# Order of first loads, of routing and scatter, router by quarters and a shared expert in 11 parts, in a two-layer kernel on one Trainium2 core

## The chip, the core and the metric

The kernel runs on one core of one Trainium2 chip. The metric is device time in microseconds (us) of one execution. The engines are TensorE (PE in the profile; PEld is its loading of weights), VectorE (DVE), ScalarE (ACT), GpSimd (POOL) and SyncE (SP), which only issues DMAs here. ScalarE and GpSimd issue DMAs too. Each engine takes its instructions strictly in order.

## The reference, cut to what matters

Two layers over 4 sequences of 512 tokens with 512 channels, all in float32. Each of the four blocks gets the normalised input, and its normalised output is added to the residual x.

```python
# layer 0, attention: a state space model of 1024 channels
conv = silu(causal_depthwise_conv4(x @ in_proj.T))
dt = softplus(einsum(conv, dt_w) + dt_b); s = scan(exp(dt*A), dt*B*conv)
x0 = ((C*s + D*conv) * sigmoid(x @ gate_proj.T)) @ out_proj.T
# layer 0, feed forward: 8 experts, 2 per token, and a shared expert of 704 columns
logits = x @ gate_weight.T; top 2 of softmax(logits)
y = sum over the 2: w * (silu(x @ gate_e) * (x @ up_e)) @ down_e      # 352 columns each
y = y + (silu(x @ sg) * (x @ su)) @ shared_down                        # 704 columns
# layer 1, attention: gated delta rule, 16 heads of 128, alpha and beta = sigmoid(x @ Wa + ba), sigmoid(x @ Wb + bb)
# layer 1, feed forward: a switch over 8 experts of width 32 per sequence
```

## The kernel before

The program has three stages, one after the other on each engine: `state_space` (L366), `experts` (L766) and `upper_layer` (L1023). A tile is 128 tokens by 512 channels (16 tiles, `x[0]` to `x[15]`); a sequence has four.

`state_space` and `upper_layer` write their work as operations with an engine, an assumed cost and a due time; `Plan.sequence` (L153) simulates the engines with these costs and fixes one order for each engine, also for SP's DMAs. `experts` is written in program order; the framework under it places each engine's instructions in an order of its own, and waits are by semaphores.

**First loads.** SP loads `x[0]` to `x[3]` (L250). ScalarE issues the constants (L252), the parameters `prm` (L369), `w_in`, `w_gate` and `w_out` (L376, L379), 14 DMAs in all. The planner then has SP load `x[4]` and on (L548) and write zeros to the buffer `xg` of routed rows in 13 DMAs (`clear`, L448), with due times only. At most 8 loads of the two queues are in flight: each later one waits for the landing of an earlier one. A sequence begins with statistics (L415), normalising (L431), transposes (L559) and copies of these by ScalarE (L569); then come the projections `w_in` and `w_gate` (L443), the convolution (L606, L617), steps through a small DRAM round trip (L481 to L530, L662), the scan and the output projection.

**Experts.** `route(b)` (L828) normalises and transposes the four tiles of sequence b and makes the router's logits with 16 matmuls of 8 columns (L836). `shared(b)` (L799) is the shared expert for one sequence: the 704 columns lie as two halves of 352 with chunks of 128, 128 and 96 (`FCH`), so 6 chunks, each with a gate and an up product of 4 matmuls (L312, 512 tokens wide), Silu on ScalarE (L808) and a multiply on VectorE (L809); then for each of the four tiles 6 matmuls down (L814), a copy (L822) and a store. The up products use 4 banks of PSUM (`mm`), the down products 2 (`tr`). Sequences 0 and 1 go route, shared, route, shared (L853); then routes 2 and 3, the top 2 and the places of all rows (L856 to L936), the scatter of 16 tiles (L939: VectorE normalises a tile into one of two buffers, GpSimd sends it to its two places by indirect DMAs, L944), and shared expert 2 (L1002). After that come 39 tiles of routed rows (`raised`, `lowered`, L954 and L980), whose expert's number is read on SP (L956) before its weights are fetched. The memory pools of this stage wait for the whole pool before them.

**Upper layer.** `shared_last` (L1139) is the shared expert of sequence 3 as planned operations; `begin(b)` (L1226) gathers the routed rows, adds, normalises and transposes, and makes alpha and beta with 16 matmuls of 32 columns and 4 for the biases (`both`, L1288). Then 8 pairs of heads for each sequence, the switch and its experts.

Of the kernel before, what the change touches and what calls it, by code (L numbers as in the profile page):

```python
# [18 lines left out]
P = 128  # L19
# [10 lines left out]
E, F, NX = 8, 352, 10  # L30
# [15 lines left out]
def _constants():  # L46
# [12 lines left out]
    parts["ones"] = np.ones((P, P))  # L59
    parts["key"] = np.broadcast_to(E - np.arange(E), (P, E))  # L60
# [174 lines left out]
def network(ctx: ExitStack, tc: tile.TileContext, a: dict, out: bass.AP):  # L235
# [16 lines left out]
    nc.scalar.dma_start(const, a["const"])  # L252
# [50 lines left out]
    def residual(pool, i, y):  # L303

        mv, rs = stats([y], EPS, "r")
        yn = pool.tile([P, D], F32, tag="xn", name="yn", bufs=2)
        normalise(yn, y, mv, rs, 0)
        nc.gpsimd.tensor_tensor(x[i], x[i], yn, ALU.add)

# [3 lines left out]

    def conv_silu(pool, dst, p, w, bias):

        cv = pool.tile([P, S], F32, tag="cv", name="cv", bufs=2)
        nc.scalar.activation(cv, p, AF.Identity, bias=bias, scale=w[:, 3:4])
        for j in range(1, 4):
            nc.vector.scalar_tensor_tensor(
                cv[:, j:], p[:, : S - j], w[:, 3 - j : 4 - j], cv[:, j:], ALU.mult, ALU.add  # L320
            )
        sg = pool.tile([P, S], F32, tag="sg", name="sg", bufs=2)
        nc.scalar.activation(sg, cv, AF.Sigmoid)
        nc.gpsimd.tensor_tensor(dst, cv, sg, ALU.mult)
# [41 lines left out]
    def state_space():  # L366
        with tc.tile_pool(name="w1", bufs=1) as wp, tc.tile_pool(name="s1", bufs=1) as sp:
            prm = wp.tile([P, a["p1"].shape[1]], F32, tag="prm", name="prm")
            nc.scalar.dma_start(prm, a["p1"])  # L369
# [3 lines left out]
            for w, name in ((w_in, "w_in"), (w_gate, "w_gate")):  # L373
                src = a[name].rearrange("(k p) c -> p k c", p=P)
                for k in range(KD):
                    nc.scalar.dma_start(w[:, k, :], src[:, k, :])  # L376
            src = a["w_out"].rearrange("(k p) d -> p k d", p=P)
            for k in range(0, NCT, 2):
                nc.scalar.dma_start(w_out[:, k : k + 2, :], src[:, k : k + 2, :])  # L379
# [26 lines left out]
            in_there = op("LD", 9.0, -9.0, lambda: None, [there])  # L406
            gate_there = op("LD", 9.0, -9.0, lambda: None, [in_there])
            out_there = op("LD", 9.0, -9.0, lambda: None, [gate_there])
# [39 lines left out]
            def clear(j, due):  # L448

                tiles = xg.rearrange("(j p) d -> p j d", p=P)  # L450
                op(
                    "SP",
                    0.42,
                    due,
                    lambda: nc.sync.dma_start(
                        tiles[:, j : j + 3, :], zero.unsqueeze(1).to_broadcast([P, 3, D])
                    ),
                )
# [78 lines left out]
            def sequence(b, due):  # L537
                xT = slot("xT", [P, KD, S], 2)
                turned = []
                for i in range(TPB):  # L540
                    xi = x[b * TPB + i]
                    ld = there
                    if b:
                        ld = op(
                            "SP",
                            0.42,
                            due - 0.8,
                            lambda xi=xi, i=i: nc.sync.dma_start(xi, x_in[b * TPB + i]),  # L548
                            landing=3.5,
                        )  # L550
# [43 lines left out]
                for half in range(2):  # L594
# [3 lines left out]
                    for ct in cts:  # L598
# [38 lines left out]
                        )  # L637
                    kept, dd = decay_steps(half, X, made, at + 0.15)
# [118 lines left out]
            for j in range(NG // 3):  # L757
                clear(3 * j, 0.8 + 0.2 * j)
# [7 lines left out]
    def experts():  # L766
        later = ctx.enter_context(ExitStack())
        lp = later.enter_context(tc.tile_pool(name="t2", bufs=1, side="right"))
        with (
            tc.tile_pool(name="w2", bufs=2) as wp,  # L770
            tc.tile_pool(name="s2", bufs=1) as sp,
            tc.tile_pool(name="e2", bufs=2) as ep,
        ):
            wr = sp.tile([P, KD, E], F32, tag="wr", name="wr")
# [24 lines left out]
            def shared(b, xT):  # L799
                acts = []  # L800
                for gu, _ in halves:
                    for lo, n in FCH:
                        act = lp.tile([P, S], F32, tag="act", name="act", bufs=2 * len(FCH))
                        pg, pu = ps("mm"), ps("mm")
                        project(pg[:n], lambda k: gu[:, k, lo : lo + n], xT)
                        project(pu[:n], lambda k: gu[:, k, F + lo : F + lo + n], xT)
                        sl = lp.tile([P, S], F32, tag="sl", name="sl", bufs=1)
                        nc.scalar.activation(sl[:n], pg[:n], AF.Silu)  # L808
                        nc.vector.tensor_tensor(act[:n], sl[:n], pu[:n], ALU.mult)  # L809
                        acts.append((act, n))  # L810
                for r in range(TPB):
                    pd = ps("tr")
                    for f, (act, n) in enumerate(acts):
                        nc.tensor.matmul(  # L814
                            pd,
                            lhsT=act[:n, r * P : (r + 1) * P],
                            rhs=halves[f // len(FCH)][1][:n, f % len(FCH), :],
                            start=f == 0,
                            stop=f == len(acts) - 1,
                        )  # L820
                    y = ep.tile([P, D], F32, tag="y", name="y")
                    nc.scalar.copy(y, pd)  # L822
                    nc.sync.dma_start(ys[b * TPB + r], y)
# [4 lines left out]
            def route(b):  # L828

                home = sp if b < B - 1 else lp  # L830
                xT = home.tile([P, KD, S], F32, tag="xT", name="xT")
                norms.append(norm_transposed(sp, xT, b))
                lg = ps("sq")[:, : TPB * E]
                for i in range(TPB):
                    for k in range(KD):
                        nc.tensor.matmul(  # L836
                            lg[:, i * E : (i + 1) * E],
                            lhsT=xT[:, k, i * P : (i + 1) * P],
                            rhs=wr[:, k, :],
                            start=k == 0,  # L840
                            stop=k == KD - 1,
                        )
# [5 lines left out]
            halves = []  # L848
            for j in range(2):
                gu = lp.tile([P, KD, 2 * F], F32, tag=f"gu{j}", name="gu")  # L850
                dn = lp.tile([P, len(FCH), D], F32, tag=f"dn{j}", name="dn")
                halves.append(fetch(gu, dn, a["gu"][j], a["dn"][j]))
            for b in range(B - 2):  # L853
                shared(b, route(b))
            xT = [route(b) for b in range(B - 2, B)]
# [83 lines left out]
            for i in range(NT):  # L939
                xn = sp.tile([P, D], F32, tag="xn", name="row", bufs=2)  # L940
                mv, rs = norms[i // TPB]
                normalise(xn, x[i], mv, rs, i % TPB)
                for k in range(2):
                    put = nc.gpsimd.indirect_dma_start(  # L944
                        out=xg,
                        out_offset=bass.IndirectOffsetOnAxis(ap=places[k][:, i : i + 1], axis=0),
                        in_=xn,
                        in_offset=None,
                        bounds_check=NG * P - 1,
                    )  # L950
                    tc.declare_no_dep(put.ins, group="put", reason="places are distinct")
                    tc.add_to_no_dep_group("put", put.ins)

            def raised(j):  # L954
# [3 lines left out]
                    a["gu"][bass.DynSlice(v + 2, 1)].rearrange("o d f -> (o d) f"),  # L958
                    a["dn"][bass.DynSlice(v + 2, 1)].rearrange("o f d -> (o f) d"),
# [42 lines left out]
            shared(B - 2, xT[0])  # L1002
# [6 lines left out]
            pool=lp, close=later.close, xT=xT[1], halves=halves, places=places, gates=gates  # L1009
# [13 lines left out]
    def upper_layer(first):  # L1023
        with (
# [56 lines left out]
            def one(v, cc):  # L1081
                return v[:, cc * P : (cc + 1) * P]
# [56 lines left out]
            def shared_last(due):  # L1139

                acts, ops = [], []
                xT, halves = first["xT"], first["halves"]
# [4 lines left out]
                def product(p, w, k, rhs, due, after, slots, stop):  # L1147
                    return op("PE", 0.88, due, lambda: mm(p(), w(), rhs(), k == 0, stop), after, slots)

                for n in range(2 * len(FCH)):  # L1150
                    gu = halves[n // len(FCH)][0]
                    at, width = FCH[n % len(FCH)]
                    act, sl = held("act", 2 * len(FCH)), held("sl", 1)
                    d, done, banks = due + 0.65 * n, [], []
                    for lo in (at, F + at):
                        p, last = bank("mm"), None
                        for k in range(KD):
# [4 lines left out]
                                lambda p=p, gu=gu, k=k, lo=lo, w=width: mm(  # L1162
                                    p()[:w], gu[:, k, lo : lo + w], xT[:, k, :], k == 0, k == KD - 1
# [6 lines left out]
                    last = op(  # L1170
                        "ACT",
                        0.63,
                        d,
# [1272 lines left out]
```

## Time and profile before

| what | us |
|---|---|
| median of 3 runs (lowest to highest) | 3107.18 (3105.93 to 3120.01) |
| the profiled execution, its time | 3114.02 |
| its span, first to last instruction | 3112.3 |
| state space, until the last output projection | 0 to 400.9 |
| experts until the first routed tile | 409.0 to 654.7 |
| routed tiles | 654.7 to 984.4 |
| upper layer | 984.4 to 3112.3 |

The granted TensorE clock was 0.958 of full speed on average, in the records either 1.0 or 0.5. In the page, "x13191" is a number of instructions; a float32 matmul makes two records. Section 2 cuts the span into 40 slices of 77.8 us, one digit each, with 9 for 90% or more. A line of a group has the line of the code, the engine, the operation, what is written from what, the shapes, the count, the total busy us, the mean ns of one, and the idle time of the engine before it with what ended that. Matmuls overlap, so the mean ns of one is longer than its share of the time. A line of waits has who waited for whom, the total us, the times and the longest. A line of a timeline has the start in us, how long it took, the engine, the line of the code and the operation, and in brackets the idle time before it and its releaser; "ACTq" is ScalarE issuing DMAs. A line of windows has the stretch, its length, for each engine the busy us and the count, then the granted clock, the DMA engines' busy share and GB/s.

### The profile page before, as it was taken

How to read it: one execution, taken by the hardware profiler on the slowest of the kernel's cores; microseconds unless marked ns; L12 is line 12 of the kernel's file. 1: busy time of each engine (PE TensorE's matmuls, PEld its weight loads, DVE VectorE, ACT ScalarE, POOL GpSimd, SP SyncE). 2: the span in 40 equal slices, each digit the busy share in tenths (PEclk: the TensorE clock that was granted, in tenths of full speed). 3: DMA queues.
4: the chain of work that ended last, by engine and by line, in shares of the span. 5: the costliest groups of instructions: out<-in, count | busy, mean ns of one | idle time of the engine just before them, and what ended most of it. 6: DMA issues, size and time to landing. Idle time of an engine off the chain costs nothing. (4 is left out here: it accounts for less than half of the span.)

```text
span 3112.3 us, 38963 instructions
## 1 busy us (share of the span) xinstructions
PE 2897.8 (93%) x13191; PEld 1623.0 (52%) x13191; DVE 1873.7 (60%) x4648; ACT 1149.7 (37%) x2398; POOL 678.7 (22%) x853
## 2 busy tenths in 40 slices
PE   6899989989999999999998989999989999999976
PEld 2344444445554455655554546555656564656532
DVE  3676730211112466777768785678877678867556
ACT  3454301111111234444444434445544544544530
POOL 0222310210001212332132232122232222221133
PEclk9899989899999999999999999899999999999998
DMA  6111120469996343443345442335443345433333
GB/s 259 56 36 42 42 72 17 153 233 321 319 316 211 88 104 93 118 102 95 77 123 161 110 114 62 80 103 166 115 130 92 90 106 139 122 75 79 84 115 115
DMA packets 288970, 383.81 MB, mean 123 GB/s; under 512 B 127586, under 2 KB 127970, under 8 KB 288514
## 3 DMA queue, kind: packets, MB, share of 16 engines
q1 hardware_dynamic: 274640, 346.07, 38.3%
q0 software_dynamic: 5120, 16.78, 1.6%
q10 hardware_dynamic: 9010, 18.46, 1.6%
q8 instruction: 105, 1.72, 0.2%
q14 instruction: 95, 0.78, 0.1%
HBM read 320.38 MB, written 60.82 MB: 122 GB/s over the span
## 5 line engine op out<-in xcount | busy, mean ns | idle before, releaser
L1085 PE MATMUL mm<-xT,wh 128*128 128x512 f32 x1536 | 775.1, 605 | 3.7 <-issue 3.0
L1448 DVE SCALAR_TENSOR_TENSOR cv<-mm,prm,cv 128x511 f32<-128x511 f32 (+2 forms) x576 | 429.0, 746 | 132.6 <-ACT cv L1437 120.9
L1085 PEld LDWEIGHTS mm<-xT,wh 128*128 128x128 f32 x1536 | 263.7, 193 | 180.4 <-issue 165.4
L1085 PE MATMUL mm<-wo,oT 128*128 128x512 f32 x512 | 262.2, 627 | 10.9 <-DVE cv L1448 9.9
L1615 DVE TENSOR_TENSOR xb<-xb,term 128x60 f32<-128x60 f32 (+24 forms) x992 | 246.7, 249 | 32.3
L1606 DVE TENSOR_TENSOR term<-lb,xb 128x60 f32<-128x60 f32 (+24 forms) x992 | 227.8, 230 | 56.6 <-DMA lb<-blocks 33.0
L1085 PE MATMUL mm<-xT,wg 128*128 128x512 f32 x512 | 261.5, 602 | 0.0
L1437 ACT ACTIVATE cv<-mm,prm 128x512 f32<-128x512 f32 x192 | 148.6, 775 | 196.5 <-PE mm L1085 194.2
L1530 POOL TENSOR_TENSOR kq<-qk,ag 128x384 f32<-128x384 f32 x128 | 121.7, 958 | 430.7 <-ACT qk L1463 278.6
L971 PE MATMUL mm<-gu,rT 128*128 128x352 f32 x624 | 190.9, 459 | 0.0
L971 PEld LDWEIGHTS mm<-gu,rT 128*128 128x128 f32 x624 | 118.2, 190 | 76.1 <-issue 17.8
L1085 PE MATMUL sq<-S,kq 128*128 128x128 f32 x768 | 150.7, 278 | 1.1 <-DVE S L1821 1.0
L1085 PEld LDWEIGHTS sq<-S,kq 128*128 128x128 f32 x768 | 124.5, 195 | 32.1 <-issue 20.4
L312 PE MATMUL mm<-xT,gu 128*128 128x512 f32 (+1 forms) x288 | 135.2, 631 | 3.5 <-DVE act L809 3.5
L1085 PEld LDWEIGHTS mm<-wo,oT 128*128 128x128 f32 x512 | 91.8, 197 | 88.6 <-issue 68.2
L1085 PE MATMUL mm<-qk 128*128 128x256 f32 x512 | 131.2, 387 | 3.9 <-ACT qk L1463 3.3
L1463 ACT ACTIVATE qk<-cv 128x512 f32<-128x512 f32 x128 | 80.7, 630 | 134.6 <-DVE cv L1448 128.8
L1085 PEld LDWEIGHTS mm<-xT,wg 128*128 128x128 f32 x512 | 91.0, 193 | 75.2 <-issue 71.2
L1085 PEld LDWEIGHTS sq<-const,vT 128*128 128x128 f32 x512 | 88.5, 193 | 75.1 <-issue 44.1
L977 DVE TENSOR_TENSOR actr<-slr,mm 128x352 f32<-128x352 f32 x39 | 20.3, 521 | 177.9 <-PE mm L971 177.9
L443 PE MATMUL mm<-xT,w_in 128*128 128x512 f32 x256 | 125.7, 615 | 1.4 <-ACT xT L569 1.4
L443 PE MATMUL mm<-xT,w_gate 128*128 128x512 f32 x256 | 123.3, 594 | 1.7 <-DVE cv L617 1.7
(277 smaller groups left out, 4754.5 us busy)
## 6 DMA issues: line engine op xcount, KB each, us to landing
gu<-in_gu SPq DMA_DIRECT2D x82, 704.0 KB
wh<-in_wh SPq DMA_DIRECT2D x192, 256.0 KB
ag<-dd SPq DMA_DIRECT2D x64, 516.0 KB
sw<-in_sw SPq DMA_DIRECT2D x96, 256.0 KB
dn<-in_dn SPq DMA_DIRECT2D x41, 512.0 KB
lb<-blocks SPq DMA_DIRECT2D x128, 128.0 KB
wg<-in_wg SPq DMA_DIRECT2D x64, 256.0 KB
wo<-in_wo SPq DMA_DIRECT2D x64, 256.0 KB
```

Of the source, the lines that this page charges most:

```text
L312: nc.tensor.matmul(dst, lhsT=w(k), rhs=xT[:, k, :], start=k == 0, stop=k == n - 1)
L443: lambda: nc.tensor.matmul(p(), lhsT=lhsT(), rhs=rhs(), start=first, stop=last),
L971: nc.tensor.matmul(dst, lhsT=rT[:, k, :], rhs=gu[:, k, lo : lo + F], start=k == 0, stop=k == KD - 1)
L977: nc.vector.tensor_tensor(act, sl, pu, ALU.mult)
L1085: nc.tensor.matmul(dst, lhsT=lhsT, rhs=rhs, start=start, stop=stop)
L1437: lambda p=p, cv=cv, j=j: nc.scalar.activation(cv(), p(), AF.Identity, bias=cb[:, j, h : h + 1], scale=cw[:, j, h, 3:4]),
L1448: lambda p=p, cv=cv, j=j, t=t: nc.vector.scalar_tensor_tensor(cv()[:, t:], p()[:, : S - t], cw[:, j, h, 3 - t : 4 - t], cv()[:, t:], ALU.mult,
L1463: lambda cv=cv, view=view: nc.scalar.activation(view(), cv(), AF.Silu),
L1530: lambda j=j: nc.gpsimd.tensor_tensor(kq()[:, j], chunk(qk()[:, j, :])[:, 1:, :], g()[:, 1:, j : j + P], ALU.mult,),
L1606: nc.vector.tensor_tensor(part(), lb()[:, i : i + 1, i + 1 :].to_broadcast([P, n, left]), xb()[:, :n, i : i + 1].to_broadcast([P, n, left] ...
L1615: nc.vector.tensor_tensor(rest, rest, part(), ALU.add)
```

## The change

- ScalarE issues no loads at the start. SP issues all: `x[0]` to `x[3]`, the 128 columns of the constants that hold the identity, `w_in`, `prm`, `w_gate`, `w_out`, the rest of the constants, then `x[4]` and on. The clears are tied in the plan to the beginnings of the sequences, and the assumed times of the loads are shorter.
- The weights of the shared expert are an array of their own (`sgu`, `sdn`), with gate and up columns cut alternately: 5 parts of 128 gate and 128 up columns, and one part of 64 gate and 64 up columns in one bank of PSUM: 11 products instead of 12. The last part goes through `raise_rest` (Silu from partitions 0 to 63 to 64 to 127, then two multiplies of 64x256, for two halves of the tokens, into two halves of the partitions), and its down product through `lower_rest` (64 rows, ahead of the other five). The down products go in pairs of tiles.
- Order: route 0, shared 0, routes 1, 2, 3, shared 1, the top 2 and the places, then shared 2 with `put_rows` called after each of its 6 parts (3 tiles each).
- The experts' router is 4 matmuls of 32 weight columns (8 real, padded), one for each quarter of the channels into its own 32 partitions, a copy by ScalarE, and 4 matmuls with a constant (`quarters`) that add the quarters. Alpha and beta are made in the same way.
- The pools of the experts wait tile by tile (`reuse_waits="tile"`).

```diff
-    nc.scalar.dma_start(const, a["const"])
+    nc.sync.dma_start(const[:, :P], a["const"][:, :P])
...
+            for w, name in ((w_in, "w_in"), (w_gate, "w_gate"), (w_out, "w_out")):
...
+                for k in range(0, w.shape[1], n):
+                    nc.sync.dma_start(w[:, k : k + n, :], src[:, k : k + n, :])
+                if w is w_in:
+                    nc.sync.dma_start(prm, a["p1"])
+            nc.sync.dma_start(const[:, P:], a["const"][:, P:])
...
+                for n in range(NS + 1):
+                    act = lp.tile([P, S], F32, tag="act", name="act", bufs=NS + 1)
+                    sl = lp.tile([P, S], F32, tag="sl", name="sl", bufs=1)
+                    p = [ps("mm") for _ in range(2 if n < NS else 1)]
+                    for j, dst in enumerate(p):
+                        lo = (2 * n + j) * P
+                        project(dst, lambda k: sgu[:, k, lo : lo + P], xT)
+                    if n < NS:
+                        nc.scalar.activation(sl, p[0], AF.Silu)
+                        nc.vector.tensor_tensor(act, sl, p[1], ALU.mult)
+                    else:
+                        for step in range(2):
+                            raise_rest(act, sl, p[0], step)
+                    acts.append(act)
+                    if between:
+                        between(n)
+                for r in range(2):
+                    pd = [ps("tr") for _ in range(2)]
+                    for n in range(2):
+                        lower_rest(pd[n], acts[NS], n, r + 2 * n)
...
+                zp, lg = ps("sq"), ps("sq")[:, : TPB * E]
+                for k in range(KD):
+                    nc.tensor.matmul(
+                        zp[k * BK : (k + 1) * BK, :], lhsT=wr[:, k, :], rhs=xT[:, k, :], start=True, stop=True
+                    )
+                zs = sp.tile([P, S], F32, tag="zq", name="zq", bufs=1)
+                nc.scalar.copy(zs, zp)
                 for i in range(TPB):
...
-            for b in range(B - 2):
-                shared(b, route(b))
-            xT = [route(b) for b in range(B - 2, B)]
+            shared(0, route(0))
+            xT = [route(b) for b in range(1, B)]
+            shared(1, xT[0])
             e, ri, hots = top2(sp, logits, NT)
...
-            for i in range(NT):
...
+            def put_rows(part):
+                for i in range(3 * part, min(3 * part + 3, NT)):
...
-            shared(B - 2, xT[0])
+            shared(B - 2, xT[1], put_rows)
...
+                def parts():
+                    for k in range(KD):
+                        mm(zq()[k * BK : (k + 1) * BK, :], wab[:, k, :], xT()[:, k, :])
+
+                z = op("PE", 1.2, due, parts, turned, [zq, zs, xT])
+                z = op("ACT", 0.6, due, lambda: nc.scalar.copy(zs(), zq()), [z], [zq, zs])
...
-                            mm(dst, xT()[:, k, i * P : (i + 1) * P], wab[:, k, :], k == 0, False)
+                        mm(dst, one(zs(), i), c("quarters"), True, False)
                         mm(dst, ones[:1, :], bab, False, True)
```

## The prediction

> **What bounds the kernel now.** I read the page first, then windows of 50 us, then the waits of PE in the stages that the change touches, then the single instructions there.
>
> ```profile
> PE 2897.8 (93%) x13191; PEld 1623.0 (52%) x13191; DVE 1873.7 (60%) x4648; ACT 1149.7 (37%) x2398; POOL 678.7 (22%) x853
> ...
> PE   6899989989999999999998989999989999999976
> ...
> PEclk9899989899999999999999999899999999999998
> ```
>
> TensorE is busy 93% of the span. So time comes off only by fewer matmul records, shorter holes of PE, or a better clock. The holes of the early stages, by what ended them (total us, times, longest), from the waits of PE over 0 to 50 and 600 to 650 us:
>
> ```profile
> PE tr L559 <- ACT xT L569: 17.3, 1, 17.3
> PE tr L559 <- DVE xn L431: 10.0, 1, 10.0
> ```
>
> ```profile
> PE tr L814 <- DVE act L809: 12.2, 2, 7.0
> PE mm L312 <- DVE act L809: 3.5, 2, 2.7
> ```
>
> The first is the start, and ScalarE's own list of instructions says why it was late:
>
> ```profile
> 24.86 2.51 ACTq L379 DMA_DIRECT2D w_out<-in_w_out  x4
> 27.40 1.28 ACT L386 ACT_TABLE_LOAD   x1 [27.40 <-DMA x<-in_x]
> 28.69 0.21 ACT L386 ACTIVATE A<-prm 128x8 f32<-128x8 f32 x1
> 28.81 1.05 ACT L569 COPY xT<-tr 128x512 f32<-128x512 f32 x2
> ```
>
> ScalarE issued 14 loads, each behind the landing of an earlier one, and could not copy the first transpose (made at 9.96) before 28.81; the first projection ran at 32.07. The second pair of holes is the scatter: in the third shared expert VectorE's multiplies (L809) stand in one queue with copies of rows that wait for the scatter's DMAs (waits of DVE, 570 to 660 us):
>
> ```profile
> DVE row L283 <- DMA xg<-row,index: 42.4, 14, 8.5
> ```
>
> The matmul groups that are priced below:
>
> ```profile
> L836 PE MATMUL sq<-wr,xT 128*128 128x8 f32 x128 | 19.8, 290 | 0.0
> ...
> L467 PE MATMUL sq<-X,prm 128*32 128x512 f32 x64 | 9.6, 605 | 0.1
> ...
> L1085 PE MATMUL mm<-xT,wblk 64*128 64x512 f32 x32 | 9.4, 679 | 0.0
> ```
>
> A float32 matmul is two records. In full stretches a 128x512 record takes 0.43 us (96 in 41.3), whether its weights are 128 or 96 wide. Eight records of a 32-wide set (L467) take 9.6/8 = 1.2 us together, and a 64-row one 9.4/32 = 0.29.
>
> **Start: -12.5 us.** All loads go to SP's queue in order of use; ScalarE issues none. The row statistics wait for prm (VectorE's first instruction), now behind x0 to x3 (1.05 MB), 0.07 MB of const and w_in (2.1 MB): 3.38 MB with prm. The slices of the DMA view show 380 to 420 GB/s from 3 us on and little before 2.3, so prm lands at 2.3 + 3.38/0.405 = 10.7, say 11.0 (before: 7.38). From prm to the fourth normalised tile took 6.9 us (7.38 to 14.27); transposes 0.85, copy 0.58 and handovers 0.3 follow: first projection at 19.6 instead of 32.07. The cover that can fail: VectorE's statistics of x4 and x5 stand ahead of the first convolution; these tiles now come last, 8.9 MB deep, at 24.3, and free VectorE at 27.8, when the first convolution (ScalarE 40.35 before) would be due at 27.9. At the 323 GB/s that the first 60 us averaged they come at 30 and the gain falls to -7; the clears that no longer stand ahead of seq. 0's dp transfers could add -1.5. PE is busy 50 of 50 us in most windows from 150 to 400, so the gain is carried on. The 13.7 us hole at 106 (VectorE's chain) and the 8.1 us one at 409 (statistics of x after the last residual) keep their instructions.
>
> **Shared experts: -10.3 us up, -1.1 down, +4.4 bubbles.** 704 columns in 11 parts instead of 12 remove 8 records each: 3 x 8 x 0.43 = 10.3 us before the routed tiles. Of the down products two pairs per expert have 64 rows; the first can run at 0.29 a record (-0.55), the second waits for the bank that ScalarE still empties: -0.4 each, bounds 0 and -1.1. New: the down products begin with the last half part, so PE waits for Silu (0.6), two 64x256 multiplies (estimate 0.42 each from 0.69 for 512) and handovers (0.3): 1.9 us for the first and third expert, 0.65 for the second, where other matmuls stand between. No row shows this wait; bounds 0 and 6, I take 4.4.
>
> **Routers of the experts: -2.1 and -6.9 us.** Each has 32 records of 8 columns; after the change 8 records of a set and 8 of 8 columns. Router 0 ran cold, 7 us of small records; it becomes 2.1 (a set at half speed) + 1.7, but part of that overlapped transposes: 409.0 to 419.2 becomes 409.0 to 417.1. Routers 1 to 3 took 5.75 + 15.1 us without the projections between; 48 transposes and handovers remain, 14 us: -6.9, bounds -3 and -9 (ScalarE's extra copy, 0.6, comes in between).
>
> **Scatter: -3.2 us.** In the built order the routing ends right behind the second expert's up products, so 20.2 us of down products and 16.2 us of the third expert's up products (four banks, one freed by ScalarE) now lie over it. But the copies are not spread between the parts: VectorE has copies 2 to 11 ahead of the first multiply of the third expert, 12 to 15 ahead of the second. Queued behind them are those multiplies, behind these PE's banks.
>
> ```profile
> 595.11 0.55 DVE L283 TENSOR_SCALAR row<-x,mv,rs 128x512 f32<-128x512 f32 x1 [8.45 <-DMA xg<-row,index]
> ...
> 626.09 0.55 DVE L283 TENSOR_SCALAR row<-x,mv,rs 128x512 f32<-128x512 f32 x1 [1.99 <-DMA xg<-row,index]
> ...
> 638.64 0.55 DVE L283 TENSOR_SCALAR row<-x,mv,rs 128x512 f32<-128x512 f32 x1 [2.32 <-DMA xg<-row,index]
> ```
>
> The first put left at 586.23: copy 2 came 8.9 us later, copy 11 39.9, copy 15 52.4. The same three sets of expert weights (6.5 MB) are fetched beside it, only held up by stores of results on SP, so I keep this pace. My clock of the new stage, with all starts as in the old trace: second up stage ends 532.5, first put 538.5, PE out of banks at 571, first multiply done 579, PE 6.9 us of work, second multiply done 591.5. Holes 7.5 + 5 = 12.5 instead of 15.7. With puts at POOL's own 1.28 us each, copy 11 comes at +27.5 and copy 15 at +38: no holes. With the 9 us per two tiles of the loaded stretch throughout, copies 11 and 15 come at +45 and +63: holes 24.
>
> **Half speed: -5.2 us.** In the experts' prologue records ran 12.9 us longer than at 0.43 (3.1, 1.7 and 8.1 in the three experts). I count 2.0 + 1.7 + 4 after it, bounds 4 and 13. The windows show why it isn't less: PE worked from 409.0 on, and the granted clock was still down:
>
> ```profile
> 410.00:420.00 10.00, 10.00 (x46) 9.48 (x45) 4.62 (x13) 3.62 (x5) 1.28 (x2) 0.50 1.04 374
> 420.00:430.00 10.00, 10.00 (x19) 4.12 (x18) 4.31 (x13) 0.60 (x1) 2.52 (x4) 0.74 0.01 3
> ```
>
> The Trainium skill, page "TensorE: Matmul & The Clock Gate", section "Part 1: The HAM clock gate (the "warmup" mystery)", has full speed return after about 3.4 us of sustained work. By that each of the two new holes would cost 1.7 us more, 3.4 in place of my 4; the row shows over 10 us where the work was small transposes, so I stay with the row.
>
> To the routed tiles (654.7 before) this makes -12.5 - 24.4 = -37.
>
> **Last shared expert and the a/b routers: -5.4 and -7 us.** The last expert loses 8 records, 3.4 us, in dense work. Each of four a/b routers has 32 records at 23.6/128 = 0.18 us, 5.9 us; it becomes a set of 1.2 and 8 records, 1.5. The first is a chain (1025.45 to 1034.5, 9.1 us, PE only) and becomes 2.1 cold + 0.9 for the copy + 4.1: -2. The other three save 3 us of PE each if PE is what lacks there: it is busy 185 to 199 of each 200 us, so -7, bounds 0 and -9.
>
> The Trainium skill, page "TensorEngine Tiling (Array Packing)", section "Key Properties", speaks against all these narrow sets: changing the tiling mode drains the engine. Of L467 the trace shows eight records from 59.99 and the next full matmul at 60.98, no hole, so I charge nothing. The page gives no price; at a whole record, 0.43 us, for each of 32 changes it would be +14 us, 3072.
>
> **Order of the upper layer: 0, bounds -12 and +12.** Its planner runs on the changed operations, and moves solves, loads and the second sequence's beginning of the first pairs; the counts of instructions stay. I know no sign.
>
> **Sum.** -12.5 - 24.4 - 5.4 - 7 = -49.3. The profiled execution took 3114.0 us (span 3112.3) and gives 3064.7; it was 0.2% above the median of 3107.2, which gives **3058**.
>
> **Rivals.**
> Scatter free of the weights: POOL's pace holds, no holes and 2.5 us less at half speed, -15: 3043. For it: SP holds back the later weights behind four stores. Against it: the same bytes in the same 22 us. 0.17.
> Scatter slow: 9 us per two tiles to the end, +12: 3070. Copies 8 to 12 came 5.1 us per pair in the old trace, against it. 0.10.
> Start without gain beyond -7 and a/b routers beside the path (-2 only): +5.5 + 7: 3070. 0.10.
> Gains given back within 0.5%: reordering and bubbles return 34 us or more: about 3097. 0.08.
> Slower: the new order of the upper layer leaves more holes. From 1200 to 3000 PE is busy 190.4 of 200 us on average and 184.6 in the worst window, the clock 0.96 and 0.91 in the worst. All nine windows as bad cost 9 x 5.8 = 52 us and 0.054 x 1800 = 97 by the clock, 3207. It decides from 65 us on, 44% of that; at 75 the time is 3133. For it: the moves begin in the first pairs; against it: from the third sequence on the order is nearly the old one. 0.06.
> The forecast itself: 0.49. A measurement here tells 0.5% (15.5 us) from no change, so faster, below 3091.6, is 0.49 + 0.17 + 0.10 + 0.10 = 0.86, within 0.08, slower 0.06. The range reaches from the free scatter less 12 to the slow one plus 12 and a little, 3030 to 3085.
>
> **What would show it.** Right: first projection near 20 us; 352 up records of shared experts in place of 384; two waits of PE on VectorE's multiply, together 8 to 16 us, in the third expert; routed tiles beginning near 618; holes in the upper layer as before. Wrong: statistics of x4 past 28 us; a first put more than 7 us behind the second up stage; a new wait at the 64-row products above 2 us; a granted clock below 0.95.

## The result and the profile after

| what | before | after |
|---|---|---|
| median of 7 runs each, same chip (lowest to highest), us | 3108.38 (3104.54 to 3121.71) | 3076.09 (3068.77 to 3089.65) |
| ratio, 95% interval | | 0.9893 (0.9868 to 0.9919) |
| profiled execution, span, us | 3112.3 | 3067.0 |
| first projection | 32.07 | 21.77 |
| first transposes of the experts | 409.01 | 401.05 |
| first routed tile | 654.71 | 617.50 |
| first matmul of the upper layer | 984.36 | 947.17 |
| mean granted clock | 0.958 | 0.967 |

The change makes the kernel 1.07% faster, 32.3 us by the medians (25 to 41 by the interval): faster, as forecast, and inside the range, but 18 us short of the 3058. The profiled execution of after is the fastest of its seven. Single executions differ along with their granted clock: it goes from 0.967 (3068.77 us) to 0.959 (3089.65 us), and 0.008 of 3067 us is 24.5 us. So the two profiles, which lie 45.3 us apart, are compared stage by stage and not by their ends alone.

The page of after:

```profile
PE 2849.9 (93%) x13031; PEld 1575.2 (51%) x13031; DVE 1882.6 (61%) x4652; ACT 1153.9 (38%) x2406; POOL 675.6 (22%) x853
...
PE   7799989899998999999898989999999999999986
...
PEclk9899999999999999999999989899989999999998
```

160 records of PE are gone and 47.9 us of its busy time; the share of the span is 93% as before.

**The start.** Waits of PE over the first 60 us, then VectorE's first instruction, then the GB/s of 40 slices of the first 14 us:

```profile
PE tr L546 <- DMA w_gate<-in_w_gate: 15.5, 1, 15.5
```

```profile
12.97 0.17 DVE L373 TENSOR_TENSOR BC<-prm 128x8 f32<-128x8 f32 x1 [12.97 <-DMA prm<-in_p]
```

```profile
GB/s 1 0 0 0 0 123 181 386 334 357 281 263 275 334 291 246 263 276 304 320 341 351 386 398 421 421 421 398 410 456 398 395 390 416 454 398 433 421 433 386
```

The wait of PE is put down to the weights of the gate, which its first transposes don't read: the 8 semaphores of the loads are used in turn, and the last one to move before a wait ends gets the name (const, which they do read, and a part of w_gate share one of them). The line of VectorE has the real cause: prm, 2 us later than forecast. The loads ran at 246 to 357 GB/s from 2.8 to 7.7 us, 303 on average, and at 386 to 456 behind that; in the kernel before the average of those same us was 393.

**The experts.** Windows of after from the first transposes to the first routed tile and over the upper layer (length, then busy us of PE, PEld, DVE, ACT, POOL, then clock, DMA share, GB/s):

```profile
401.05:617.50 216.45, 200.26 (x540) 90.02 (x541) 46.64 (x119) 32.62 (x53) 37.40 (x41) 0.96 0.29 108
...
947.17:3067.00 2119.83, 1965.74 (x10465) 1136.60 (x10463) 1519.87 (x3964) 897.91 (x2020) 533.80 (x692) 0.96 0.39 106
```

The first took 245.7 us before, at a clock of 0.90. Waits of PE in it, and PE's timeline in the third shared expert:

```profile
PE mm L308 <- DVE row L286: 12.2, 2, 7.8
PE tr L294 <- DVE xn L286: 8.3, 2, 7.9
PE tr L874 <- DVE act L869: 2.3, 2, 1.1
```

```profile
542.51 16.47 PE L308 MATMUL mm<-xT,sgu 128*128 128x512 f32 x38
566.74 8.67 PE L308 MATMUL mm<-xT,sgu 128*128 128x512 f32 x16 [7.75 <-DVE row L286]
579.90 15.70 PE L308 MATMUL mm<-xT,sgu 128*128 128x512 f32 x32 [4.49 <-DVE row L286]
```

The two holes of the scatter stand where the forecast put them (7.5 + 5), and the wait at the 64-row products is 1.1 us in two of the three experts. Routed tiles begin at 617.5; 618 was forecast.

**The upper layer.** The same window of before:

```profile
984.36:3112.30 2127.94, 1985.82 (x10537) 1161.70 (x10535) 1511.58 (x3963) 896.23 (x2016) 537.09 (x692) 0.96 0.39 106
```

PE's busy time fell by 20.1 us and its idle time (length less busy) rose from 142.1 to 154.1. Waits of PE in this window, before and then after:

```profile
PE tr L1085 <- DVE xx L1653: 32.6, 22, 3.9
...
PE sq L1085 <- ACT u L1794: 9.2, 13, 1.6
```

```profile
PE tr L1117 <- DVE xx L1713: 41.9, 25, 5.2
...
PE sq L1117 <- ACT u L1854: 13.5, 19, 1.6
```

Both are waits on the way through the small solves of the delta rule: xx is made from what comes back from DRAM (the tiles solved and yi in the kernel), u from PE's own short products. "Holes in the upper layer as before" was one of the prediction's signs of being right, and it did not come.

### The profile page after: what moved, and what is told of

It is laid out like the page before. It is cut to its first block, busy times and chain, and to the rows that moved or that the text cites. A ratio compares the mean times of both kernels' runs of the same rounds, so it can differ in the third digit from the quotient of the medians.

```text
span 3067.0 us, 38661 instructions
## 1 busy us (share of the span) xinstructions
PE 2849.9 (93%) x13031; PEld 1575.2 (51%) x13031; DVE 1882.6 (61%) x4652; ACT 1153.9 (38%) x2406; POOL 675.6 (22%) x853
## 5 line engine op out<-in xcount | busy, mean ns | idle before, releaser
L1675 DVE TENSOR_TENSOR xb<-xb,term 128x60 f32<-128x60 f32 (+24 forms) x992 | 250.8, 253 | 32.3
L1290 POOL DMA_INDIRECT got<-yg,index x32 | 36.2, 1131 | 436.3 <-DMA yg<-yo 367.1
L308 PE MATMUL mm<-xT,sgu 128*128 128x512 f32 x264 | 119.9, 611 | 12.2 <-DVE row L286 12.2
```

The lines of the kernel that those rows point to most:

```text
L308: nc.tensor.matmul(dst, lhsT=w(k), rhs=xT[:, k, :], start=k == 0, stop=k == n - 1)
L1290: nc.gpsimd.indirect_dma_start(out=to(), out_offset=None, in_=yg, in_offset=bass.IndirectOffsetOnAxis(ap=places[k][:, n : n + 1], axis=0), ...
L1675: nc.vector.tensor_tensor(rest, rest, part(), ALU.add)
```

## The experiments

Theory: the start, the shared experts, the routers and the scatter give what the stages show (37 us to the routed tiles), and the missing 10 us and more are the a/b routers (alpha and beta) of the upper layer, whose saving turned into idle time. Rivals: the start's gain is lost later; another order of the upper layer costs the time; the scatter's DMAs rather than VectorE's queue make the holes. The new order of routing and the pools that wait tile by tile were not taken back alone.

| kernel | runs | faster than before, us (medians) | ratio, 95% interval |
|---|---|---|---|
| e1_loads | 7 | 9.0 | 0.997 (0.9954 to 0.9986) |
| e2_old_ab | 4 | 40.7 | 0.9865 (0.985 to 0.988) |
| e3_plan_only | 11 | -2.4 | 1.0005 (0.9993 to 1.0018) |
| e4_in_place | 5 | 57.3 | 0.9811 (0.9786 to 0.9835) |
| e9_ab_cost | 6 | 33.4 | 0.9884 (0.9858 to 0.991) |
| after_again | 6 | 34.7 | 0.9882 (0.9852 to 0.9912) |
| e6_prm_first | 6 | 44.1 | 0.9851 (0.9825 to 0.9876) |
| e10_best | 6 | 40.7 | 0.9872 (0.9844 to 0.9899) |
| e7_old_route | 7 | 28.2 | 0.992 (0.9892 to 0.9947) |
| e8_12_products | 6 | 33.7 | 0.9904 (0.9876 to 0.9932) |
| e10_again | 6 | 62.2 | 0.9808 (0.9781 to 0.9834) |
| e11_place_prm | 6 | 52.0 | 0.9831 (0.9803 to 0.9859) |

An interval is 4 to 9 us either way, so a term of 5 to 8 us is read from the stages of the profiled executions, and the median only says whether it arrives. The upper layer of all these executions, from its first matmul to the end, by the same windows; the us at half clock are from the clock records of each trace:

| kernel | a/b routers | length | idle PE | at half clock |
|---|---|---|---|---|
| before | old | 2127.9 | 142.1 | 189 |
| e1_loads | old | 2128.3 | 143.7 | 189 |
| e3_plan_only, other order | old | 2131.5 | 145.0 | 188 |
| e2_old_ab | old | 2125.5 | 142.1 | 182 |
| e10_best | old | 2123.2 | 146.7 | 169 |
| e10_again | old | 2131.4 | 142.7 | 203 |
| after | new | 2119.8 | 154.1 | 162 |
| after_again | new | 2127.2 | 152.2 | 183 |
| e4_in_place | new | 2134.5 | 154.8 | 199 |
| e6_prm_first | new | 2128.7 | 151.4 | 184 |
| e7_old_route | new | 2128.6 | 153.4 | 182 |
| e8_12_products | new | 2121.8 | 144.7 | 182 |
| e9_ab_cost, other order | new | 2127.4 | 157.8 | 169 |
| e11_place_prm | new | 2131.6 | 151.3 | 196 |

**e1_loads**: before with the new loads alone.

```diff
-    nc.scalar.dma_start(const, a["const"])
+    nc.sync.dma_start(const[:, :P], a["const"][:, :P])
...
+            for w, name in ((w_in, "w_in"), (w_gate, "w_gate"), (w_out, "w_out")):
...
+                clear(3 * j, 0.8 + 0.2 * j, begun[min(j // 4, B - 1)])
```

> The kernel before with the new loads alone (all on SP, in order of use, clears tied to the sequences); PE's order stays that of before. My step: the first projection comes near 21.8 us, as in the changed kernel, 10.3 earlier than before, and since PE is nearly full from 150 us on, 8 to 10 us arrive at the first transposes of the experts (409.0 before) and at the end: 8 to 10 us faster than before (0.3%). Rival: the later holes of the state space (near 106 and 409 us) or the clock take the gain back: within 3 us of before.

9.0 us faster. First projection at 21.7, experts from 400.00 (9.0 earlier than before), first routed tile at 645.45 (9.3 earlier):

```profile
400.00:645.45 245.45, 229.46 (x628) 112.88 (x629) 46.13 (x116) 30.33 (x49) 37.42 (x41) 0.90 0.26 96
```

This stretch is as long as before (245.7). The start's gain is carried to the end; the rival falls.

**e2_old_ab**: after with the old a/b routers.

```diff
-                z = op("PE", 1.2, due, parts, turned, [zq, zs, xT])
-                z = op("ACT", 0.6, due, lambda: nc.scalar.copy(zs(), zq()), [z], [zq, zs])
...
+                        for k in range(KD):
+                            mm(dst, xT()[:, k, i * P : (i + 1) * P], wab[:, k, :], k == 0, False)
...
+                z = op("PE", 6.0, due, both, turned, [bps, xT, nb])
```

> The changed kernel with the a/b routers of the upper layer as before (16 matmuls of 32 columns each). The groups of the changed kernel show 11.8 us less PE work in these routers, and its upper layer 12.3 us more idle PE. Theory A, my step (the saved records count): 7 to 10 us slower than the changed kernel, 23 to 25 us faster than before. Theory B (the saving comes with a new order of the upper layer whose holes give it back): within 3 us of the changed kernel, with some 12 us less idle PE in the upper layer.

40.7 us faster than before, where after had 32.3 and (after_again) 34.7: not slower than after; that it is faster the intervals don't show. The a/b groups of e2_old_ab, then those of after:

```profile
L1117 PE MATMUL sq<-prm,xT 128*128 128x32 f32 x128 | 25.0, 352 | 0.0
L1117 PE MATMUL sq<-prm,const 1*128 1x32 f32 x32 | 8.7, 360 | 0.0
```

```profile
L1117 PE MATMUL sq<-prm,const 1*128 1x32 f32 x32 | 7.4, 313 | 0.0
L1117 PE MATMUL sq<-const,row 128*128 128x32 f32 x32 | 7.1, 308 | 0.7 <-ACT row L1347 0.7
L1117 PE MATMUL tr<-xT,prm 128*32 128x512 f32 x32 | 6.0, 833 | 0.7 <-ACT xT L1162 0.7
```

33.7 us of busy PE against 20.5: the records are saved. But with the old ones the wait for xx is that of before again:

```profile
PE tr L1117 <- DVE xx L1706: 33.7, 23, 3.8
...
PE sq L1117 <- ACT u L1847: 12.0, 16, 1.8
```

Idle PE is 142.1 against 154.1. Theory A falls, and theory B fits: what the new routers save comes back as idle time (the time came out 6 to 8 us below that of after, where B had it within 3). Whether the order or the missing records do it, this run can't tell, since both changed.

**e3_plan_only**: before, another order of the upper layer.

```diff
-                z = op("PE", 6.0, due, both, turned, [bps, xT, nb])
+                z = op("PE", 3.0, due, both, turned, [bps, xT, nb])
```

> The kernel before with one assumed cost in the planner of the upper layer changed (a/b router 3.0 instead of 6.0 us): the same instructions in another order from the first pairs of heads on. Theory A (the order of the upper layer alone moves the time, my bounds were 12 us either way): over 6 us from before, and the idle time of PE after 1000 us changes by as much. Theory B (order without effect): within 3 us of before.

The time is the same within 0.2%, idle PE 145.0 against 142.1. This order costs nothing.

**e9_ab_cost**: after, another order of the upper layer.

```diff
-                z = op("PE", 1.2, due, both, [z], [bps, zs, nb])
+                z = op("PE", 5.0, due, both, [z], [bps, zs, nb])
```

> The changed kernel with the assumed cost of the second half of the a/b router set to 5.0 instead of 1.2 us in the planner of the upper layer: the same instructions in another order. It tells why the upper layer has 154 us of idle PE with the new a/b routers and 142 with the old ones. If the order is the cause: idle PE near 142 to 146 in the upper layer, and the time 6 to 10 us below the changed kernel. If the removed records are missing as filler beside the waits for the small solves: idle again 150 to 158 and the time within 4 us of the changed kernel.

3074.3 us against 3073.0 of after_again in the same group; idle PE 157.8:

```profile
PE tr L1117 <- DVE xx L1713: 42.2, 28, 5.0
...
PE sq L1117 <- ACT u L1854: 13.1, 17, 1.6
```

A second order of the new records has the same waits, a second order of the old ones (e3_plan_only) hasn't. So the idle time comes with the new routers, not with one unlucky order. The totals alone don't carry this: e8_12_products runs the upper layer of after in the same order and has 144.7 us of idle PE. One place does. In the 200 us that begin 1400 us behind the layer's first matmul, with the last of the four a/b routers at their beginning, PE is idle for 4.8 to 7.6 us in all eight executions with the new routers (5.9 in e8_12_products) and for 0.4 to 1.1 in all six with the old ones. Its waits there, in after and then in e2_old_ab:

```profile
PE tr L1117 <- DVE xx L1713: 3.5, 2, 2.8
PE sq L1117 <- DVE S L1881: 1.7, 1, 1.7
PE mm L1117 <- DVE cv L1508: 1.4, 1, 1.4
PE tr L1117 <- ACT xx L1725: 0.9, 2, 0.7
```

```profile
PE tr L1117 <- issue: 0.4, 1, 0.4
PE mm L1117 <- issue: 0.2, 1, 0.2
```

With the records gone PE reaches the solves earlier and waits for them. That place holds about 5 of the 8.8 us between the two means of idle time. A wait for xx some 1285 us behind the layer's first matmul adds a part: it is 4.0 to 5.2 us in six of the eight and 2.6 to 2.8 in the other two (e7_old_route, e8_12_products) and in all six with the old routers, so more than the routers decides there, and what it is stays open. A plan that fills these places was not found.

**after_again**: the changed kernel once more.

> The changed kernel once more, timed beside the others of this group, since single executions of it lie 20 us apart. Its ratio to the kernel before should be 0.989 again, 0.987 to 0.991; the upper layer should again have 154 us of idle PE within 2, whatever its clock is.

0.9882; routed tiles at 615.99; idle PE of the upper layer 152.2, with the same holes in the experts. All begins of stages repeat within 2 us. The upper layer is 7.4 us longer than in the profile of after, with 21 us more at half clock.

**e4_in_place**: rows normalised in place.

```diff
-                    xn = sp.tile([P, D], F32, tag="xn", name="row", bufs=2)
+                    xn = x[i]
```

> The changed kernel with the scattered rows normalised in place in x (not needed afterwards) instead of in two buffers, so that VectorE's copies wait for no DMA; all copies stand ahead of the third expert's multiplies. My step (the holes of 12.2 us come from copies that wait for buffers): both holes go, routed tiles begin near 604 instead of 617.5, 12 to 14 us faster than the changed kernel, 44 to 47 faster than before. Rival (the scatter's DMAs are the limit): PE then waits for the last put ahead of the first routed tile, and the gain is under 5 us.

57.3 us faster than before. The 16 copies now run at 470 to 482 us, long before the first put, and wait for nothing. Waits of PE from 380 to 620, and one window while the puts run:

```profile
PE tr L294 <- DVE xn L286: 8.6, 3, 7.9
PE tr L874 <- DVE act L869: 2.3, 2, 1.1
```

```profile
540.00:550.00 10.00, 10.00 (x25) 4.43 (x24) 0.69 (x1) 1.18 (x2) 7.56 (x9) 1.00 1.04 416
```

Both holes are gone with the DMA engines as full as before. Routed tiles begin at 601.65; the stretch from the experts' first transposes is 201.07 instead of 216.45 us, 15.4 shorter. The buffers were the cause, and the rival falls. Of the 22 to 25 us between the medians of this kernel and of after, the trace explains these 15; the rest is within the intervals.

The place stays close to another limit: ScalarE's third Silu came at 568.52, after 16.1 us without work behind DMAs that it issues itself, and PE waited 0.2 us for it.

What the change says of the scatter, rows sent between the parts of one expert, the built order doesn't do. In the trace of after ten of VectorE's copies run from 535.19 to 565.54 us, ahead of the third expert's first multiply (566.00), and the last four ahead of its second (579.16).

**e6_prm_first**: prm ahead of w_in.

```diff
+            nc.sync.dma_start(prm, a["p1"])
             for w, name in ((w_in, "w_in"), (w_gate, "w_gate"), (w_out, "w_out")):
...
-                if w is w_in:
-                    nc.sync.dma_start(prm, a["p1"])
```

> The changed kernel with the parameters (prm) loaded ahead of w_in instead of behind it. In the changed kernel prm landed at 12.97 us and the first instructions of VectorE and ScalarE waited for it. If prm is what the start waits for: prm lands near 7.5, the first projection comes at 15.5 to 17 instead of 21.8, and 4 to 6 us arrive at the end. Rival: w_in or x3 is then last, or the first convolution waits for x4's statistics: first projection at 19 or later, or less than 2 us at the first transposes of the experts.

VectorE begins 5.8 us earlier, the first projection comes at 15.97, routed tiles at 611.41 (617.50 and 615.99 in the two executions of after), and the median is 9.5 us below after_again:

```profile
7.17 0.17 DVE L372 TENSOR_TENSOR BC<-prm 128x8 f32<-128x8 f32 x1 [7.17 <-DMA prm<-in_p]
```

prm was what the start waited for.

**e7_old_route**: after with the old router of the experts.

```diff
-                    nc.tensor.matmul(
-                        zp[k * BK : (k + 1) * BK, :], lhsT=wr[:, k, :], rhs=xT[:, k, :], start=True, stop=True
-                    )
...
+                    for k in range(KD):
+                        nc.tensor.matmul(
+                            lg[:, i * E : (i + 1) * E],
+                            lhsT=xT[:, k, i * P : (i + 1) * P],
+                            rhs=wr[:, k, :E],
```

> The changed kernel with the experts' router as before (16 matmuls of 8 columns per sequence, without ScalarE's copy). My step priced the four routers at 2.1 + 6.9 us, bounds 3 and 9 on the last three: the stretch from the first transposes of the experts to the first routed tile is 7 to 11 us longer than the 216.5 of the changed kernel, and the time 6 to 11 us above it. Rival: the routers lay beside transposes and statistics, and the stretch grows by less than 4 us.

The stretch is 6.4 to 6.7 us longer than in the two executions of after, the time 4 to 6.5 by the medians:

```profile
399.27:622.41 223.14, 209.85 (x604) 104.37 (x605) 46.66 (x119) 30.20 (x49) 37.33 (x41) 0.94 0.28 105
```

PE's busy time is 9.6 us longer, its idle time 2.9 shorter (holes of the scatter 10.7 instead of 12.2). The routers count, for some 6.5 of the 9 us. This execution also had 10 us more at half clock in the stretch (28.5 against 18.6), so a part of the 6.5 is clock.

**e8_12_products**: after with 12 products in the first three shared experts.

```diff
-                    p = [ps("mm") for _ in range(2 if n < NS else 1)]
+                    p, m = [ps("mm") for _ in range(2)], P if n < NS else P // 2
...
+                        project(dst[:m], lambda k: sgu[:, k, lo : lo + m], xT)
...
+                            lhsT=act[:n, i * P : (i + 1) * P],
+                            rhs=sdn[:n, m, :],
```

> The changed kernel with the shared expert in 12 products for the three sequences ahead of the routed tiles (the last part as 64 gate and 64 up columns in two banks, its down product last, as in the kernel before); the fourth sequence in the upper layer keeps the 11. My step: 3 x 8 records x 0.43 = 10.3 us more up products, less the two bubbles of 1.1 us that the changed kernel shows: the stretch from the experts' first transposes to the first routed tile grows by 7 to 10 us, the time by as much. Rival: the third expert's records are hidden in the holes of the scatter and the stretch grows by 4 to 6 us only.

The stretch is 7.7 to 8.0 us longer than in after:

```profile
399.54:623.99 224.45, 216.31 (x564) 90.79 (x564) 45.89 (x116) 32.80 (x53) 37.46 (x41) 0.96 0.28 104
```

```profile
PE mm L308 <- DVE act L798: 6.5, 3, 3.0
```

This is not a pure test: the framework here placed VectorE's copies between the multiplies, so the holes are 6.5 us in three pieces, and the down products are unpaired again, with the 64 rows last. PE's busy time is 16.0 us longer than in after, its idle time 8.1 shorter. The 11 products are worth about 8 us net, with the holes they leave open. The median (33.7 us faster than before) doesn't tell it from after; the upper layer of this execution was 5.4 us shorter than that of after_again.

**e10_best**: in place, prm first, old a/b routers together.

```diff
-                    xn = sp.tile([P, D], F32, tag="xn", name="row", bufs=2)
+                    xn = x[i]
...
+            nc.sync.dma_start(prm, a["p1"])
             for w, name in ((w_in, "w_in"), (w_gate, "w_gate"), (w_out, "w_out")):
...
+                z = op("PE", 6.0, due, both, turned, [bps, xT, nb])
```

> The changed kernel with three edits together: rows normalised in place, prm ahead of w_in, and the a/b routers of the upper layer as before. If the three add up: 15 (holes of the scatter and half speed there) + 5 (start) + 0 to 8 (order of the upper layer) faster than the changed kernel, 50 to 62 us faster than before. If the start's gain is lost on the way, or the upper layer's gain was chance: 45 to 50.

A miss: 40.7. The third expert had a hole that none of the theories has. Waits of PE; then ScalarE's Silus, VectorE's first multiply of that expert, and two windows:

```profile
PE mm L308 <- DVE act L798: 13.2, 1, 13.2
```

```profile
546.59 0.60 ACT L797 ACTIVATE sl<-mm 128x512 f32<-128x512 f32 x1 [11.21 <-remote]
564.26 0.60 ACT L797 ACTIVATE sl<-mm 128x512 f32<-128x512 f32 x1 [17.08 <-DVE act L798]
```

```profile
563.48 0.69 DVE L798 TENSOR_TENSOR act<-sl,mm 128x512 f32<-128x512 f32 x1 [44.67 <-remote]
```

```profile
540.00:550.00 10.00, 10.00 (x25) 4.37 (x23) 0.00 (x0) 0.60 (x1) 7.57 (x9) 1.00 1.03 413
550.00:560.00 10.00, 1.02 (x3) 0.19 (x1) 0.00 (x0) 0.00 (x0) 7.87 (x9) 0.77 0.96 387
```

PE began the products at 534.55. In e4_in_place the first Silu followed PE's beginning by 2.8 us and the multiply by 6.3; here by 12.0 and 28.9, with products long made and no copy in the queue, until 4 us after GpSimd had sent the last put (559.29). "remote" means that the trace names no releaser.

**e10_again**: the same file once more.

> The same three edits as in e10_best once more. There the first execution showed one hole of 13.2 us in the third expert, for which neither VectorE's copies nor a buffer was the cause, and the parts did not add up (41 us faster than before instead of 50 to 62). If the hole belongs to the program: a hole of 8 to 14 us at the same place, and again 38 to 45 us faster than before. If it was chance: no hole, the stretch from the experts' first transposes to the first routed tile at 199 to 203 us, and 50 us or more.

62.2 us faster than before, no hole, the stretch 200.83 us, routed tiles at 595.06. Waits of PE from 385 to 612:

```profile
PE tr L294 <- DVE xn L286: 8.6, 3, 7.9
PE tr L873 <- DVE act L868: 2.3, 2, 1.1
```

The hole doesn't belong to the program: the kernel is the same, and in the experts' stretch the traces show the same order on VectorE, ScalarE and GpSimd. All six executions of e10_best (3064.1 to 3077.5 us) lie above all six of e10_again (3046.2 to 3058.0), so it probably stood in all of the first group. Its cause stays open.

**e11_place_prm**: the two edits without the old a/b routers.

```diff
-                    xn = sp.tile([P, D], F32, tag="xn", name="row", bufs=2)
+                    xn = x[i]
...
+            nc.sync.dma_start(prm, a["p1"])
             for w, name in ((w_in, "w_in"), (w_gate, "w_gate"), (w_out, "w_out")):
```

> The changed kernel with the rows normalised in place and prm ahead of w_in, its own a/b routers kept. Alone these gave 57 and 44 us against the kernel before, where the changed kernel gave 33 to 35. If they add: 62 to 68 us faster than before, routed tiles near 596. If a hole as in e10_best comes with the earlier prm, whatever the a/b routers: 40 to 50, and a hole of 8 to 14 us in the third expert.

52.0 us (44 to 61 by the interval), below the 62 expected. In the trace the two add: routed tiles at 595.77, 21.7 earlier than in after, against 15.4 and 6.1 alone, and no hole:

```profile
394.65:595.77 201.12, 196.71 (x541) 88.87 (x542) 44.73 (x119) 32.53 (x53) 37.72 (x41) 0.98 0.30 116
```

My 62 to 68 added medians, and these lay 7 to 10 us (e4_in_place) and 3 to 6 us (e6_prm_first) beyond what the stages of their traces explain. e4_in_place, e10_again and e11_place_prm beat both kernels; their intervals overlap, so which of them is best is not settled.

## Why the prediction was right, and where it was not

Right in sign and range. That the routed tiles begin 37.2 us earlier, where 37 was forecast, is in part luck: the start gave 4.5 us less than forecast and the experts' stretch 4.8 us more. The miss of the sum lies behind the routed tiles.

- **Start, -12.5: -10.3 at the first projection, -8.0 to -9.8 at the experts.** The mechanism holds (e1_loads alone: -9.0). The number that failed is the landing of prm, 12.97 instead of 11.0. About half of this is the rate: 3.38 MB had moved by 11.75 us, not by 10.7. The rest lies behind that sum: 0.3 MB of w_gate moved ahead of prm's last packet (12.47), and VectorE began 0.5 us after it. x4's statistics came at 26.07, before the 28 named as a limit. The 323 GB/s taken as the slow case, the mean of the first 60 us, averages in some 9 us without loads; over the first 50 us it is 385.
- **Shared experts, -10.3 - 1.1 + 4.4 = -7.0: about -8** by e8_12_products, which is not a pure test. The bubbles are 1.1 us each, 2.3 in all, not 4.4.
- **Routers, -2.1 - 6.9: -6.5** (e7_old_route), inside what the bounds of 3 and 9 on the second part allow.
- **Scatter, holes 12.5: 12.2**, at the two places named; the first put 4.5 us behind the second up stage (6.0 forecast), copies 11 and 15 at +39.3 and +52.4 (+39.9 and +52.4 forecast). The pace was taken from the old trace and held.
- **Half speed, -5.2: about -6.7.** Counted record by record from each start to the next, those of the shared experts ran 12.6 us over 0.43 each in before and 5.9 in after (1.4, 0.7 and 3.8 in the three experts, where 2.0, 1.7 and 4 were forecast).
- **The experts' stretch, -24.4: -29.2.** PE is idle for 16.2 us in it before and after, where the forecast had 1.2 more after, so all of it is busy time. By the same count the up products take 15.3 us less (10.3 by 24 records fewer, the rest by the clock), the router records 10.2, the down products 2.9 and the transposes 0.8. These are somewhat more than forecast, by the same mechanisms.
- **Last expert and a/b routers, -12.4: -1.7. This is the step that failed**, and in it the -7 of three a/b routers. I priced them at their records because PE is busy 185 to 199 of 200 us, and took the average share of busy time for a proof that nothing ends later there. Behind the last of them PE reaches the solves earlier and waits. With the new routers the upper layer's idle PE is 152.5 us in the mean of eight executions, with the old ones 143.7 in the mean of six. The lengths are 2127.5 with the new routers, 2126.7 with the old ones and the new shared expert, and 2129.2 with both old (means of eight, three and three; single ones spread by 15 us). So the last expert's records gave 2.5 of the 3.4 forecast, as far as this spread tells, and the a/b routers nothing. The rival with these routers "beside the path" had 0.10, and it was this half of it that came. The first router's matmuls take 7.3 us instead of 9.1 (-2 forecast), but they begin 0.9 later, behind the copy of the last tile, and the result comes 0.9 earlier from the start of the layer.
- **Order of the upper layer, 0 with bounds of 12:** right. Two other orders of the same instructions moved the time by 0.05% and 0.02%.

Sum: -37.2 to the tiles and -1.7 behind them make -39, inside the 25 to 41 us of the interval.

The windows with the two holes, at their ends:

```profile
560.00:570.00 10.00, 3.26 (x4) 1.51 (x5) 2.78 (x5) 0.60 (x1) 7.75 (x8) 0.66 0.62 220
...
580.00:590.00 10.00, 10.00 (x20) 4.35 (x21) 1.38 (x2) 1.73 (x3) 3.74 (x5) 0.83 0.44 154
```

The second is 0.17 x 10 x 2 = 3.4 us at half clock from the moment PE resumed, with large records; the first hole's half-clock time went on 3.1 us into the work, by the clock records (566.74 to 569.87). In the Trainium skill, page "TensorE: Matmul & The Clock Gate", section "Part 1: The HAM clock gate (the "warmup" mystery)", full speed returns after about 3.4 us of sustained work. The forecast took 4 us of loss for both holes from a row of small transposes; half of these times, 1.6 and 1.7, is the loss here, which agrees with the page. All half-clock stretches in the records of this trace but one are multiples of 3.41 us, so the agreement can't be finer than that.

## What to carry to other kernels

A PE that is busy 93% of the time still has stretches where something else ends last: price a removed record there by the wait beside it, not by the engine's average. Before scattering work between others, look at the built order: here two buffers in a queue of VectorE cost 12 us of holes and 3.5 of busy time at half clock, and using the old data's own place removed them. Load the smallest thing that everybody waits for first.

## What was not expected of the hardware

- With all loads issued by SP they ran at 303 GB/s from 2.8 to 7.7 us and at 413 from there to 14 us (e1_loads: 306 and 403). In the kernel before, where SP and ScalarE issue and the loads come in another order, it was 393 and 379. Whether the one issuing engine or the order makes the slow first us, no run tells.
- In one group of executions ScalarE and VectorE began 12 and 29 us behind PE where e4_in_place had 3 and 6, with the DMA engines full in both; the same file in another group had no such hole. No row tells why.
- The time at half clock in the upper layer differs from execution to execution of nearly the same instructions, 162 to 203 us, and with it the time by up to 20 us.
